# A graph-network kernel: what stands between encoder attention and the encoder MLP, rearranged

## The chip, the core and the metric

The kernel runs on one core of a Trainium2 chip. The metric is device time in microseconds (us) for one execution of the whole program. The core has five engines that run their own instruction streams and wait for each other through semaphores: TensorE (PE in the profile, with its weight loads as PEld), VectorE (DVE), ScalarE (ACT), GpSimd (POOL) and SyncE (SP). Here POOL and SP mostly issue DMA transfers. TensorE writes to PSUM, a small memory of eight banks, from which VectorE and ScalarE read.

## What is computed

Four graph layers run one after the other on 2708 nodes with 512 features each, with a dense 0/1 adjacency matrix; after each layer the input is added and a layer norm taken. The change lies in the first layer, and in a preparation for the fourth that is done in the middle of the first:

```
# layer 0 (cut)
Xw   = per head h (4 heads of 128): X_h @ W_h
att  = masked softmax of sigmoid(f1_i + f2_j), mask = adjacency
Xc   = att @ Xw                                  # encoder attention: "first pass"
Xn   = (Xc - mean) * rsqrt(var + 1e-6) * gamma + beta      # batch norm over the nodes
h    = elu(Xn @ Wm.T + bm) + Xn                  # encoder MLP
emb  = batch norm of h
Y    = att @ emb ...                             # decoder attention: "second pass"
# layer 3 (cut)
query, key = x @ Wq + bq, x @ Wk + bk
a    = query @ key.T / sqrt(512) + ...; softmax(a) @ value
```

Since a row of the softmax does not change when a constant is added to the row, layer 3 needs of its projections only the product M = Wq Wk^T / sqrt(512) and the vector u = Wk bq / sqrt(512).

## The kernel before, in words

All data is fp32. Features of layer 0 are held transposed, as `ft[128 features, 4 blocks, 2708 nodes]`. The two attention passes are written as `attention_pass`. Each has four parts (two halves of the nodes times two pairs of heads), and each part 22 steps, one for each block of 128 source nodes. A step forms a tile t of attention weights: two Tanh on ScalarE (L406, one for each head), a product with the mask on VectorE (L414), an Exp on ScalarE (L415). TensorE then multiplies: L438 in the first pass (22 small products for each step), L456 in the second. In the second pass some tiles are read back from DRAM instead of being formed, and VectorE counts zeros for some steps (L355). Two steps run ahead in the first pass; in the second, four tile buffers set how far the forming can run ahead.

At the end of each part of the first pass, `keep` (L636) divides the sums in PSUM by their row totals on VectorE (L656 to L658) into `rows`, and `turn` (L666) transposes the rows on TensorE (L675) into the banks of the second head of the pair. VectorE copies them into `ft` (L695), and later takes batch statistics of them (L697). The row totals are transposed as well (L683), copied (L685) and sent to DRAM as `rs_d` by POOL (L687, L691). SP reads them back as `rb` for the second pass (L333), after its `f1b` (L513). VectorE's first use of `rb` is `linked` (L884).

After the first pass the following is written down:

- `batch_scale` and `batch_shift` (L588, L602; the root is L111, on ScalarE) turn the statistics into `scale1` and `shift1`, so that Xn = scale1 * ft + shift1.
- Wq and Wk, loaded in two halves each by SP (L719), are transposed by TensorE in groups of four (L732) through two banks, psm0 and psm1, in turn. ScalarE copies each group into the end of `emb` (L737).
- `merged(c)` multiplies the transposed weights (L748); ScalarE scales and stores the result (L755). merged(0) comes first, 1 and 2 later. The fourth is made elsewhere.
- `small_product` (L608) multiplies a vector with a 512x512 matrix on TensorE as a row (L611), copies the row (L614), and turns it into a column (L616). It is called for `shift1` with the MLP weights (ps_shift), to give the MLP a bias that contains the shift, and for bq with Wk (ps_u), to give `uq`.
- The MLP weights `enc_w` are scaled in place by `scale1`, two blocks on VectorE (L777), two on ScalarE (L773). So the MLP reads the features before normalization.
- POOL writes the transposed weights and the merged product to DRAM (L781, L782, L786).

The MLP loop goes over six chunks of 452 or 450 nodes. For each chunk TensorE makes four output blocks of four products (L805) in pairs of banks, of which there are three. For each output block ScalarE takes an Exp (L575), VectorE makes the elu of it (L580, L582), adds `scale1 * ft` in place (L818; the rest of the shift is in the next batch norm, which removes any constant), and takes statistics (L821). Finished columns of `ft` are transposed by TensorE (L826) and copied to `emb` by ScalarE (L827).

The order on each engine is not the order of the text: a scheduler places the instructions by its own estimate of times, and each engine then works strictly in the order it was given. `tc.issue_after(x)` tells it to place an instruction after x. Waits on PSUM and SBUF are derived by tile. In the first pass a tile `both[q]` holds one bank of each of the two heads, so that the two banks are one tile to those waits; the fourth bank of each head is a tile by itself.

Of the kernel before, what the change touches and what calls it, by code (L numbers as in the profile page):

```python
# [8 lines left out]
F32 = mybir.dt.float32  # L9
# [3 lines left out]
AF = mybir.ActivationFunctionType  # L13
# [16 lines left out]
def gnn_stack_kernel(  # L30
# [149 lines left out]
    uq = const.tile([P, C], F32, name="uq")  # L180

    feats = ExitStack()
    pf = feats.enter_context(tc.tile_pool(name="feat", bufs=1, side="right"))
    with ExitStack() as l0:
# [36 lines left out]
        def project(att, psum):  # L221
# [90 lines left out]
            def rest(step):  # L312

                with tc.issue_after(step.ins):
# [8 lines left out]
                    copies(f2h[:, NT - 1, :])  # L323
                    nc.vector.tensor_scalar(bm1, prm_sb[:, MB_DEC, :], 1.0, None, ALU.subtract)

# [15 lines left out]
        def attention_pass(values, first, att, psum, finish, f1b=None, blocks=(), spread=None, rest=None):  # L341
# [23 lines left out]
            def form(hf, p, jt, att, prepare, f1b, tv):  # L365
# [49 lines left out]
                exp = nc.scalar.activation(tv, tv, AF.Exp, scale=0.5)  # L415
                if not opening:
                    opening[1] = tanh
# [182 lines left out]
        ready = [None]  # L600
# [7 lines left out]
        def small_product(ps, w, v, row):  # L608

            for c in range(C):  # L610
                nc.tensor.matmul(  # L611
                    ps[:1, :F], v[:, c : c + 1], w[:, c, :], start=(c == 0), stop=(c == C - 1)
                )
            nc.vector.tensor_copy(row, ps[:1, :F])  # L614
            for o in range(C):
                nc.tensor.matmul(  # L616
                    ps[:, o : o + 1],
                    row[:, o * P : (o + 1) * P],
                    ones[:1, 0:1],
                    start=True,  # L620
                    stop=True,
                )
            return ps[:, :C]


        stats = stats_tile("stats_a", 8)[:, :, : TURNS * NHALF]
        bias = p0.tile([P, 2, C], F32, name="enc_bias")
        with (
# [4 lines left out]
            mlp_w = []  # L633
            ft = feat_tile("ft")

            def keep(hf, p, po, later):  # L636
                h0, w = HSPAN[hf]
                if hf == 0 and p == 0:
                    mlp_w.append(load_mlp(enc_wT, "enc_w"))
                kept = []  # L640
# [25 lines left out]
                def turn(k):  # L666

                    h = HP * p + k
                    rows, rc = kept[k]
                    for b in range(TURNS):  # L670
                        slots = range(b * QUAD, min(NB, (b + 1) * QUAD))
                        bank = po[1][(TURNS * k + b) % (HB + 1)]
                        for r in slots:
                            i0, m = NODES[hf][r]
                            nc.tensor.transpose(  # L675
                                bank[:, r % QUAD * P : r % QUAD * P + m],
                                rows[:m, r, :],
                                ident[:m, :m],
                            )
                        c0 = b * BANK  # L680
                        cw = min(w, c0 + BANK) - c0
                        if b + 1 == TURNS:
                            nc.tensor.transpose(bank[:NB, BANK - P :], rc, ident)  # L683
                            sm = att.tile([NB, P], F32, tag="sm", name="sm")
                            nc.vector.tensor_copy(sm, bank[:NB, BANK - P :])  # L685
                            full = (NB - 1) * P
                            nc.gpsimd.dma_start(  # L687
                                rs_d[h, h0 : h0 + full].rearrange("(r i) -> r i", i=P),
                                sm[: NB - 1],
                            )  # L690
                            nc.gpsimd.dma_start(  # L691
                                rs_d[h : h + 1, h0 + full : h0 + w], sm[NB - 1 :, : w - full]
                            )
                        dst = ft[:, h, h0 + c0 : h0 + c0 + cw]
                        nc.vector.tensor_copy(dst, bank[:, :cw])  # L695
                        later.append(
                            lambda dst=dst, n=TURNS * hf + b: nc.vector.bn_stats(  # L697
                                stats[:, h, n, :], dst
                            )
                        )  # L700

                return [lambda k=k: turn(k) for k in range(HP)]

            attention_pass(xw, True, att, psum, keep, f1b, blocks, spread, rest)
            scale1, mean1 = batch_scale(stats, G_ENC, "bn1")
            shift1 = batch_shift(scale1, mean1, B_ENC, "bn1")


# [17 lines left out]
            for k, wt in enumerate((wqT, wkT)):  # L726
                for o in range(C):
                    slot = o % 2
                    tp = psum.tile([P, BANK], F32, tag=f"psm{slot}", name="tp_w", bufs=1)
                    tp = tp.rearrange("p (c d) -> p c d", c=C)  # L730
                    for c in range(C):
                        nc.tensor.transpose(  # L732
                            tp[:, c, :],
                            raws[2 * k + c // half][:, c % half, o * P : (o + 1) * P],
                            ident,
                        )
                    nc.scalar.copy(wt[:, o, :], tp.rearrange("p c d -> p (c d)"))  # L737
        with (
# [6 lines left out]
            def merged(c):  # L745
                ps = psum.tile([P, F], F32, tag="misc", name="ps_m", bufs=2)
                for o in range(C):
# [6 lines left out]
                    )  # L754
                nc.scalar.activation(mqk[:, c, :], ps, AF.Copy, scale=qscale)  # L755

            merged(0)


            (enc_w,) = mlp_w  # L760
# [22 lines left out]
            for c in range(1, C - 1):  # L783
                merged(c)
# [1335 lines left out]
```

## Time and profile before

| | us |
|---|---|
| median of 3 runs | 3179.41 (3178.1 to 3179.55) |
| profiled execution: device time | 3173.57 |
| profiled execution: span in the trace | 3171.7 |
| TensorE busy in the span | 3095.8 (98%) |
| VectorE busy | 2050.0 (65%) |
| ScalarE busy | 1347.0 (42%) |

The shares are means over stages that differ much. Layer 0 lies in the first 1090 us or so: the first attention pass ends at 522, the second begins at 644. What lies between is the subject here. A busy TensorE is not TensorE at its peak, since matmuls are pipelined; the granted clock (PEclk) and the weight loads tell more.

### The profile page before, as it was taken

Reading aid. Unit: us, or ns where it says so; the run is one execution under the profiler, and the core shown is the slowest. Engines: PE = TensorE matmul, PEld = TensorE weight load, DVE = VectorE, ACT = ScalarE, POOL = GpSimd, SP = SyncE. Lnnn points to the kernel's source line nnn. Section 1 sums busy time; section 2 is a strip of 40 time slices with the busy share of each in tenths; the row PEclk is TensorE's granted clock in tenths of the full one; section 3 lists DMA queues with packets and bytes.
Section 4 is the critical chain, followed back from the end, with each engine's and each line's share of the span. In section 5 each row is a group of like instructions: output and inputs, shape, how many; then the busy total and the mean of one; then the engine's idle time right before and its main releaser. Section 6 shows DMA issues by size and latency. Waiting matters only on the chain.

```text
span 3171.7 us, 39566 instructions
## 1 busy us (share of the span) xinstructions
PE 3095.8 (98%) x15176; PEld 2349.5 (74%) x15176; DVE 2050.0 (65%) x3819; ACT 1347.0 (42%) x1615; POOL 163.5 (5%) x282
## 2 busy tenths in 40 slices
PE   8899999999999999999999999999999999999999
PEld 7898897444444446885578888777768888888886
DVE  7968975776686684444167667767535555555565
ACT  7898896477867552001133333444301111111111
POOL 1101100000000000000011110000110000000000
PEclk9999999999999999999999999999999999999999
DMA  7866865156455413541154445566431111111111
GB/s 279 304 223 235 298 236 186 45 166 232 172 175 190 173 62 99 144 126 44 41 150 141 139 146 150 157 180 176 128 101 40 50 50 52 51 50 50 50 46 33
DMA packets 203635, 425.81 MB, mean 134 GB/s; under 512 B 20798, under 2 KB 134562, under 8 KB 197622
## 3 DMA queue, kind: packets, MB, share of 16 engines
q1 hardware_dynamic: 179454, 319.92, 33.0%
q0 software_dynamic: 23552, 101.26, 8.7%
q8 instruction: 119, 1.95, 0.2%
q10 hardware_dynamic: 440, 2.10, 0.2%
q14 instruction: 70, 0.57, 0.1%
HBM read 325.88 MB, written 95.87 MB: 133 GB/s over the span
## 4 chain that ended last, share of the span: by engine, by line
PE 77%; issue 11%; DVE 6%; ACT 3%; DMA 2%; POOL 1%; SPq 0%; POOLq 0%; DVEq 0%; ACTq 0%
PE po L1571 19%; PE ps_s L1366 18%; PE po L456 9%; PE ps_nb L1169 7%; PE po L438 7%; PE ps_wide L1219 4%; PE ps_sup L1777 2%; PE ps_mlp L805 2%; PE ps_hid L131 2%; DVE t L414 2%; PE ps_v L131 2%; PE ps_dec L936 2%; ACT t L406 1%; ACT t L415 1%; DMA kept<-t 1%
## 5 line engine op out<-in xcount | busy, mean ns | idle before, releaser
L414 DVE SCALAR_TENSOR_TENSOR t<-t,a 128x2708 f32<-128x2708 f32 (+1 forms) x152 | 450.4, 2975 | 175.3 <-ACT t L406 169.1
L438 PE MATMUL po<-xw,t 128*128 128x129 f32 (+2 forms) x3872 | 441.9, 280 | 36.3 <-ACT t L415 23.4
L438 PEld LDWEIGHTS po<-xw,t 128*128 128x128 f32 (+2 forms) x3872 | 434.1, 191 | 43.7 <-ACT t L415 35.2
L406 ACT ACTIVATE t<-f1b,f2h 128x1354 f32<-128x1354 f32 (+1 forms) x304 | 414.4, 1412 | 60.1 <-PE po L456 31.5
L1366 PE MATMUL ps_s<-q,hT 128*128 128x256 f32 (+1 forms) x1848 | 405.5, 372 | 0.0
L415 ACT ACTIVATE t<-t 128x2708 f32<-128x2708 f32 (+1 forms) x152 | 371.2, 2452 | 78.0 <-DVE t L414 75.4
L1571 PE MATMUL po<-sup,e 128*128 128x256 f32 (+1 forms) x1512 | 398.3, 384 | 5.6 <-DVE c L1652 2.8
L456 PE MATMUL po<-t,emb 128*128 128x452 f32 (+3 forms) x1056 | 396.2, 544 | 4.8 <-ACT t L415 4.7
L1366 PEld LDWEIGHTS ps_s<-q,hT 128*128 128x128 f32 x1848 | 339.2, 190 | 49.8 <-issue 5.1
L456 PEld LDWEIGHTS po<-t,emb 128*128 128x128 f32 (+1 forms) x1056 | 192.7, 189 | 201.5 <-issue 189.1
L1571 PEld LDWEIGHTS po<-sup,e 128*128 128x128 f32 (+1 forms) x1512 | 264.4, 185 | 59.9 <-issue 19.8
L1571 PE MATMUL po<-held,T 128*128 128x256 f32 x1200 | 293.7, 380 | 0.0
L1571 PEld LDWEIGHTS po<-held,T 128*128 128x128 f32 x1200 | 226.8, 190 | 31.4 <-issue 0.9
L1972 DVE SCALAR_TENSOR_TENSOR e<-a_cols,ps_s 128x512 f32<-128x512 f32 (+1 forms) x121 | 79.5, 657 | 233.5 <-PE ps_s L1366 229.8
L1366 PE MATMUL ps_s<-hT 128*128 128x256 f32 (+2 forms) x968 | 213.7, 372 | 0.7 <-ACT sup L1784 0.7
L1366 PEld LDWEIGHTS ps_s<-hT 128*128 128x128 f32 x968 | 174.9, 190 | 29.3 <-issue 4.4
L1169 PE MATMUL ps_nb<-hid_hi,at 128*128 128x512 f32 x484 | 185.5, 390 | 0.4 <-DVE at L1161 0.4
L1169 PE MATMUL ps_nb<-hid_lo,at 128*128 128x512 f32 x462 | 179.9, 389 | 0.0
L1874 ACT ACTIVATE a_score<-a_score,neg_big 128x512 f32<-128x512 f32 (+3 forms) x131 | 88.6, 683 | 194.5 <-DMA a_score<-in_adj_dram 94.2
L1476 ACT ACTIVATE e<-e 128x512 f32<-128x512 f32 (+1 forms) x187 | 113.8, 616 | 118.2 <-DVE e L1475 117.9
L1964 ACT ACTIVATE q<-ps_wide,uq 128x256 f32<-128x256 f32 (+1 forms) x44 | 20.5, 466 | 335.7 <-PE ps_wide L1219 335.7
L1571 PE MATMUL po<-sup,T 128*128 128x256 f32 x480 | 142.5, 380 | 0.0
(275 smaller groups left out, 3842.8 us busy)
## 6 DMA issues: line engine op xcount, KB each, us to landing
a<-adj_d SPq DMA_DIRECT2D x108, 677.0 KB
a_cols<-in_adjT_dram SPq DMA_DIRECT2D x200, 256.0 KB
a<-in_adjT_dram SPq DMA_DIRECT2D x42, 677.0 KB
adj_d<-a POOLq DMA_DIRECT2D x42, 677.0 KB, 5.9
kept<-t POOLq DMA_DIRECT2D x20, 1354.0 KB, 7.0
t<-kept SPq DMA_DIRECT2D x20, 1354.0 KB
raw<-in_adjT_dram SPq DMA_DIRECT2D x105, 256.0 KB
a_score<-in_adjT_dram SPq DMA_DIRECT2D x55, 256.0 KB
```

What stands on the lines that cost most here:

```text
L131: nc.tensor.matmul(ps[:n], xt[:, c, :n], w[:, c, :], start=(c == 0), stop=(c == C - 1))
L406: tanh = nc.scalar.activation(tv[:, k, :], f1b[k][:n, :w], AF.Tanh, bias=f2h[:n, jt, h : h + 1], scale=0.5,)
L414: step = nc.vector.scalar_tensor_tensor(tv, tv, GUARD, ab, ALU.add, ALU.mult)
L415: exp = nc.scalar.activation(tv, tv, AF.Exp, scale=0.5)
L438: nc.tensor.matmul(po[k][b][:m, s * DR : (s + 1) * DR], t[own : own + n, k, i0 : i0 + m], values[own : own + n, jt, HP * p + k, :], start= ...
L456: nc.tensor.matmul(po[HB * k + q][:, :qw], values[r : r + n, jt, h * P : (h + 1) * P], t[r : r + n, k, q0 : q0 + qw], start=(place == 0), ...
L1169: nc.tensor.matmul(pos[it][:n], at, half[:, jt, :], start=(jt == 0 and k == 0), stop=(jt == NT - 1),)
L1219: nc.tensor.matmul(ps[:, :width], w(c, o), xt(c), start=(c == 0), stop=(c == C - 1),)
L1366: nc.tensor.matmul(ps[:, jb, i:w], keys[:, c, j : j + P], st["q"][:, c, i:], start=(c == 0), stop=(c == C - 1),)
L1476: return nc.scalar.activation(e, e, AF.Exp)
L1571: nc.tensor.matmul(po[bank][rows, half, :], lhsT, rhs, start=(k == 0 and half == 0) if first is None else first, stop=last, skip_group_che ...
L1874: return nc.scalar.activation(a, a, AF.Identity, bias=neg_big[: a.shape[0]], scale=1.0e30)
```

## The change

It has five parts, all between the first attention pass and the MLP, with three small preparations earlier.

1. Features are normalized in place. ScalarE writes scale1 * ft + shift1 over `ft`, one chunk ahead of the MLP's matmuls (`normal`). The MLP's weights are no longer scaled, its bias is bm itself, `less` (bm - 1) is made at the start of the kernel, and the residual add becomes a plain add.
2. `small_product` is gone. VectorE computes `uq` by four products of Wk's rows with a broadcast bq, each with a sum over the row. bq is first written to DRAM by POOL, early in the first pass, and read back by SP with a broadcast, into a buffer of `f1b`.
3. The weight transposes use the four banks of the last part's first head, and stand in a fixed order with the last part's `turn`, which is cut into its three banks (`seam`). Three of the six feature copies of that part (those of the second head) go from VectorE to ScalarE.
4. `early_root` takes a root of a constant after the last Exp of the first pass.
5. The three merged products are made one after the other, before the MLP.

The same diff, cut to its core:

```diff
+    bq_d = dram.tile([C, P], F32, name="bq_d")
...
+                    nc.gpsimd.dma_start(bq_d.rearrange("c p -> p c"), prm_sb[:, Q_B, :])
                     nc.vector.tensor_scalar(bm1, prm_sb[:, MB_DEC, :], 1.0, None, ALU.subtract)
+                    nc.vector.tensor_scalar(less, prm_sb[:, MB_ENC, :], 1.0, None, ALU.subtract)
...
                 exp = nc.scalar.activation(tv, tv, AF.Exp, scale=0.5)
+                last_exp[:] = [exp]
...
-                def turn(k):
+                final = hf == NHALF - 1 and p + 1 == H // HP
+
+                def turn(k, b):
...
+                    copy = nc.scalar.copy if final and k + 1 == HP else nc.vector.tensor_copy
...
+                    copy(dst, bank[:, :cw])
...
+                if final:
+                    last_turn.append(turn)
+                    return []
...
-            scale1, mean1 = batch_scale(stats, G_ENC, "bn1")
-            shift1 = batch_shift(scale1, mean1, B_ENC, "bn1")
...
-            for k, wt in enumerate((wqT, wkT)):
-                for o in range(C):
-                    slot = o % 2
-                    tp = psum.tile([P, BANK], F32, tag=f"psm{slot}", name="tp_w", bufs=1)
...
+            bq = att.tile([P, HW], F32, tag="f1b", name="bq", bufs=HP + 1)
+            nc.sync.dma_start(
+                bq[:, :F], bq_d.rearrange("c p -> (c p)").partition_broadcast(P)
+            )
+            for c in range(C):
+                nc.vector.scalar_tensor_tensor(
+                    bq[:, F : 2 * F],
+                    raws[2 + c // half][:, c % half, :],
+                    qscale,
+                    bq[:, :F],
+                    ALU.mult,
+                    ALU.mult,
+                    accum_out=uq[:, c : c + 1],
+                )
+
+            def weights(k, o, b):
+                tp = last_po[0][b]
...
+                nc.scalar.copy((wqT, wkT)[k][:, o, :], tp)
+                return done
+
+            early_root = small.tile([P, 1], F32, tag="ready", name="early_root")
+            with tc.issue_after(last_exp[0].ins):
+                nc.scalar.activation(early_root, ones, AF.Sqrt)
+            banks4 = [HB] + list(range(HB))
+            turn = last_turn[0]
+            seam = [lambda o=o: weights(0, o, banks4[o]) for o in range(3)]
+            seam += [lambda: turn(0, 0), lambda: weights(0, 3, banks4[3])]
+            seam += [lambda: turn(0, 1), lambda: weights(1, 0, banks4[0])]
+            seam += [lambda: turn(0, 2), lambda: weights(1, 1, banks4[1])]
+            seam += [lambda: turn(1, 0), lambda: weights(1, 2, banks4[2])]
+            seam += [lambda: turn(1, 1), lambda: weights(1, 3, banks4[3])]
+            seam += [lambda: turn(1, 2)]
+            done = None
+            for work in seam:
+                with tc.issue_after(done.ins) if done else nullcontext():
+                    done = work()
+            for work in last_later[0]:
+                work()
+            scale1, mean1 = batch_scale(stats, G_ENC, "bn1")
+            shift1 = batch_shift(scale1, mean1, B_ENC, "bn1")
...
-            merged(0)
...
-            pm = small_product(
...
-            for c in range(1, C - 1):
+            for c in range(C - 1):
                 merged(c)
...
-            pu = small_product(
...
+            def normal(ci):
+                c0, w = CHUNKS[ci]
+                for c in range(C):
+                    cols = ft[:, c, c0 : c0 + w]
+                    nc.scalar.activation(
+                        cols,
+                        cols,
+                        AF.Identity,
+                        bias=shift1[:, c : c + 1],
+                        scale=scale1[:, c : c + 1],
+                    )
+
+            normal(0)
             turned = 0
             for ci, (c0, w) in enumerate(CHUNKS):
+                if ci + 1 < NCH:
+                    normal(ci + 1)
...
                     r = elu(
-                        att, pss[o][:, :w], w, bias[:, 0, o : o + 1], bias[:, 1, o : o + 1]
-                    )
-                    nc.vector.scalar_tensor_tensor(
-                        dst, dst, scale1[:, o : o + 1], r, ALU.mult, ALU.add
-                    )
+                        att, pss[o][:, :w], w, prm_sb[:, MB_ENC, o : o + 1], less[:, o : o + 1]
+                    )
+                    nc.vector.tensor_tensor(dst, dst, r, ALU.add)
                     nc.vector.bn_stats(stats[:, o, ci, :], dst)
```

## The prediction, made before the changed kernel was run

> **What bounds the kernel now.** I read the stage table first, then the order of time inside the stage that the change touches, then the waits. All times count from the start of the profiled execution. Busy time of each engine in four stretches (first attention pass, second half; the seam between it and the encoder MLP; the MLP; the start of the second pass):
>
> ```profile
> core 0: us, PE busy (x) PEld busy (x) DVE busy (x) ACT busy (x) POOL busy (x), PEclk, DMA share, GB/s
> 390.00:522.00 132.00, 126.71 (x1152) 125.55 (x1150) 86.46 (x89) 115.91 (x69) 6.83 (x13) 1.00 0.64 225
> 522.00:561.00 39.00, 33.04 (x110) 15.26 (x109) 23.94 (x53) 22.04 (x24) 5.79 (x10) 0.82 0.52 183
> 561.00:644.00 83.00, 82.82 (x272) 43.16 (x271) 63.50 (x97) 32.06 (x46) 0.57 (x1) 1.00 0.10 32
> 644.00:700.00 56.00, 55.63 (x165) 27.75 (x165) 41.63 (x41) 46.16 (x35) 1.05 (x2) 1.00 0.52 164
> ```
>
> TensorE is full before and after the seam. In the 39 us of the seam its clock averages 0.82, its weight loads fill only 15 us, and no engine is full: a chain of small steps. Because TensorE is full on both sides, every microsecond taken from the seam should end the kernel earlier. The seam in TensorE's own order:
>
> ```profile
> 522.22 0.60 PE L732 MATMUL tp_w<-ident,wq 128*128 128x128 f32 x4
> ...
> 530.73 1.11 PE L732 MATMUL tp_w<-ident,wq 128*128 128x128 f32 x4 [0.68 <-ACT emb L737]
> 532.52 1.12 PE L732 MATMUL tp_w<-ident,wk 128*128 128x128 f32 x4 [0.68 <-ACT emb L737]
> 534.31 1.11 PE L732 MATMUL tp_w<-ident,wk 128*128 128x128 f32 x4 [0.68 <-ACT emb L737]
> 536.30 5.90 PE L748 MATMUL ps_m<-emb 128*128 128x512 f32 x8 [0.88 <-ACT emb L737]
> 542.14 3.59 PE L611 MATMUL ps_shift<-enc_w,bn_shift 128*1 128x512 f32 x8
> 545.66 1.98 PE L748 MATMUL ps_m<-emb 128*128 128x512 f32 x4
> 548.68 1.05 PE L616 MATMUL ps_shift<-ones,emb 1*128 1x1 f32 x8 [1.04 <-DVE emb L614]
> 549.66 7.11 PE L748 MATMUL ps_m<-emb 128*128 128x512 f32 x12
> 556.71 3.59 PE L611 MATMUL ps_u<-emb,prm_sb 128*1 128x512 f32 x8
> 560.23 1.78 PE L805 MATMUL ps_mlp<-ft,enc_w 128*128 128x452 f32 x4
> 561.95 1.05 PE L616 MATMUL ps_u<-ones,emb 1*128 1x1 f32 x8
> 562.92 10.88 PE L805 MATMUL ps_mlp<-ft,enc_w 128*128 128x452 f32 x28
> ```
>
> Two small products stand on this path, with two records to each fp32 matmul. Transposes alternate with ScalarE copies in steps of 1.8 us. The first MLP matmul starts at 560.23, interrupted once for 0.97 (561.95 to 562.92), so the MLP starts in effect at 561.2. From there it runs without a gap to the first matmul of the second pass at 643.74: 82.5 us. ScalarE at the same place:
>
> ```profile
> 533.67 0.59 ACT L737 COPY emb<-tp_w 128x512 f32<-128x512 f32 x1 [1.21 <-PE tp_w L732]
> 534.28 1.28 ACT L111 ACT_TABLE_LOAD   x1
> 535.57 0.20 ACT L111 ACTIVATE bn_scale<-bn_scale 128x4 f32<-128x4 f32 x1
> ```
>
> VectorE had the variance ready at 533.1, and the root ended at 535.8, behind a copy and a table load; the shift was complete at 536.57.
>
> **What the Trainium skill says.** "TensorE: Matmul & The Clock Gate", Part 1, says an idle array drops to half clock and needs about 3.4 us of work to come back, and Part 4 says that transposes do not count as such work. The trace agrees: four transposes take 0.66 us at 529.40 but 1.11 at 530.73, and matmul records of L748 start 0.85 us apart until 540.7 and 0.43 after; between 551.1 and 554.5 they fall to 0.85 again, after the gap and the tiny matmuls at 547.6 to 549.7. "ScalarE: Activation LUTs", What ACT_TABLE_LOAD costs, gives 1283 ns for a load; its Table sets section says identity and copy are in every set. The trace shows 1.28 us and copies with no load around them. "PSUM — Partial Sum Buffer", PSUM bank collisions, says engines are kept apart on one bank even when both only read; the trace shows it as VectorE's L580 waiting 16.1 us in all for the Exp L575 on the same bank.
>
> **The change part by part.**
>
> Small products gone from TensorE. ps_shift: 3.59 + 1.05, with a wait of 1.04 before its second half; ps_u: 3.59 + 1.05. Together 10.3 us, all on the path. Their helpers on VectorE (L614 twice 0.67, the bias sums) and the enc_w scaling (0.49 twice on VectorE, 1.32 on ScalarE) go too.
>
> The query bias on VectorE: four products of 128x512 with an accumulator. The nearest row is L582 at 0.625 for 452, so I estimate 0.72 each, 2.9 in all. They stand after the memsets (512.02), before the normalization of the rows, and need the last wk load: issued at 509.14, and the DMA view in half-microsecond slices shows its 0.52 MB moving from 509.5 to 512.0. VectorE idles until 519.97, so 515 to 516 leaves 4 us spare: nothing. If the load came 4 us later it would cost one for one. The bq load on SP stands right behind a transfer issued at 385.61 and waits for the last Tanh on an old f1b buffer, which ended by 384.9; SP is idle afterwards until 400. Its 0.26 MB could hold the transfer that ScalarE waits for at 398.5 by 0 to 0.7; I take 0. The scattered write of bq_d (512 pieces of 4 bytes) falls in POOL's idle time before 37.63 (8.8 us); no row is like it; wqT_d, also 512 pieces, takes 0.75 to issue and 2.7 to land. Bounds 0 to 1.5; I take 0.
>
> Transposes over four banks. In the built program 11 ScalarE copies stand in a row (8 weights, 3 of features that VectorE loses). The waits are by tile, and a tile holds the banks of both heads, so the second weight group waits until VectorE has read the second head out of it (523.7 in the trace). Bounds: 522.9 plus 11 x 0.55 (start to start of L827's pairs) is 529.0; the old pace of 1.7 a copy would give 541. Walking the order with those waits, I get weights at 522.9, 524.3 and 524.95, then one copy every 0.55 to 0.6, the last at 530.8 because it waits for VectorE's small copy: it ends at 531.2. The first merged matmul then starts at 531.2 instead of 536.30.
>
> Scale and shift. VectorE loses three copies (1.6 start to start). Its unbroken chain ended at 532.97; I take 532.0, since it now waits for ScalarE's last copy. The early root has loaded the table in the idle time after the last Exp (514.5), so the rest is six small operations, 1.2 us: shift at 533.2 (before 536.57).
>
> Merged products back to back: 24 records, cold for 4.4 us (5 records at 0.85), 19 at 0.43: 12.5 us, so they end at 543.7. MLP matmuls start there instead of at 561.2: 17.5 us earlier. As a check: 10.3 removed, 5.1 earlier start, about 1.7 for the second cold stretch gone: 17.1.
>
> Normalization on ScalarE: 24 in-place Identity operations of 128x452. The nearest row is L1874, in place, biased, 0.72 for 512; I take 0.60 start to start (bounds 0.55 and 0.72). In the built order 21 of them and three 0.6 us copies of ps_m stand before the first Exp. Three normals end at 535.0; the first copy waits for the first merged product (537.2); then five, a copy, four, and the last copy when the merged products end (544.3); nine more to 549.7; the Exp table load 1.28; first Exp done 551.7. TensorE has the first chunk's features at 538.5, so it is not held there. VectorE waits: its first elu starts 8 us after TensorE's start, 7.3 before.
>
> VectorE in the MLP. Per output block 0.60 + 0.53 + 0.55 + 0.54 = 2.2 us (start to start; the add has no per-row scale now). Before, three second-pass products and two of their counts (2.9 and 1.56 us) were done ahead of the first elu, in the seam's gaps. Now all four products stand among the elus. TensorE's transposes of chunk 2 stand after the first half of chunk 3: 56 matmuls x 0.76 plus 7.75 blocks x 0.5 = 46.4, at 590.1. VectorE must by then have done 12 elus, three products and three counts: 26.4 + 8.7 + 4.7 = 39.8, so 591.5. That is 1.4 late, and about 1.5 more goes in small waits earlier (a chunk-1 add behind a count, a transpose buffer behind a Tanh). I take 3.0 us of TensorE stall; bounds 0 and 8.
>
> On POOL, wkT_d (1 MB) now goes ahead of the last row sums rs_d, and SP's f1b and rb wait for rs_d. Before, rb landed 10.9 us after its issue at 535.92. If rs_d lands by 536 to 541, rb lands at 545 to 552; the mask from it stands before the first elu: 0 to 2 us, inside the bound above.
>
> Sum: 17.5 - 3.0 = 14.5 us. The second pass starts with four tiles ready, as before, and is full on TensorE, so it keeps the gain. The profiled execution took 3173.57 (span 3171.7), so 3159.1; the median of the runs is 5.8 above it, so 3179.41 - 14.5 = 3164.9.
>
> **The rivals.**
> Little stall: the merged products stay at full clock (2.2 better) and VectorE keeps up. For it: the stages are balanced within 1.4 us. Against: clock falls at 530.7 in the trace. Gain 17 to 20, time 3161.
> VectorE as the bound of the MLP: normals at 0.72, a late rb, and Tanh pairs in front of Exps add up to 8 us of stall. For it: 76 us of VectorE work between first elu and end against 82.5 on TensorE, in an order fixed at build time. Against: the slack is regained in the last two chunks. Gain 9, time 3170.
> Slower: the first Exp behind the normals comes so late that TensorE stands still with its six banks full. It decides when the MLP loses more than 17.5 us; the first Exp would have to end at about 566, that is 0.68 us more for each of the 21 normals, 1.3 us each. Against: L1874 shows 0.72 for a longer row. Time then 3182.
> The gain is lost later: second-pass tiles late, TensorE waits at its start. The stretch 644 to 700 has ScalarE at 46 of 56 us, so it could take some, not all: time 3175.
>
> **How the numbers follow.** Forecast 0.52, little stall 0.17, VectorE bound 0.18, lost later 0.08, slower 0.05. A measurement of this kernel tells about 0.2%, 6.4 us, from no change; the first three cases lie beyond it: 0.87 less a little for tails, faster 0.86; lost later gives no change, 0.09; slower 0.05. The range takes in both ends of the unknown costs: 3159 to 3173.
>
> **What would show it.** L111 without a table load and the shift near 533; merged products in one run from about 531, once cold; the first MLP matmul near 544 and the first second-pass matmul near 629. The forecast is wrong if the MLP stretch is over 90 us, if TensorE waits for ScalarE before its first MLP matmul, or if the first attention pass ends later than 522.4.

## The result, and the profile after

The changed kernel takes 3167.33 us (median of 7 runs, 3162.98 to 3173.58), the kernel before 3178.10 (median of 7 in the same comparison, 3174.19 to 3179.72). The ratio of the means is 0.9969, with a 95% interval of 0.9959 to 0.9979: faster by 9.9 us, interval 6.7 to 13.0 (the medians lie 10.8 apart). The forecast was a gain of 14.5. The profiled execution took 3164.28 (span 3162.3), 9.3 less than the one before.

Both profiled executions have a clear mark: TensorE's first transpose of wq, when the first pass ends, at 522.22 before and 529.95 after. All intervals below are counted from it. First the stage table of the changed kernel (columns as in the forecast):

```profile
core 0: us, PE busy (x) PEld busy (x) DVE busy (x) ACT busy (x) POOL busy (x), PEclk, DMA share, GB/s
390.00:530.00 140.00, 133.61 (x1200) 132.41 (x1199) 96.53 (x102) 123.62 (x74) 8.44 (x16) 0.99 0.66 227
530.00:550.00 20.00, 17.63 (x83) 10.65 (x81) 10.31 (x35) 14.67 (x26) 3.32 (x6) 1.00 0.45 158
550.00:634.00 84.00, 82.36 (x263) 41.55 (x262) 69.13 (x102) 51.69 (x66) 3.32 (x4) 1.00 0.22 79
```

The seam took 39 us before; it takes 20 now, at a clock of 1.00 (0.82 before). The MLP has more ScalarE (51.7 us, before 32.1) and more VectorE in it, and TensorE is a little less full there. TensorE's own order in the timeline (start, duration, line, names, records; in brackets the idle time before it and what ended it):

```profile
529.95 0.60 PE L738 MATMUL po<-ident,wq 128*128 128x128 f32 x4
531.53 1.33 PE L738 MATMUL po<-ident,wq 128*128 128x128 f32 x8 [0.98 <-DVE rows L646]
...
537.69 0.27 PE L673 MATMUL po<-ident,rc 128*11 128x128 f32 x1
539.33 10.57 PE L776 MATMUL ps_m<-emb 128*128 128x512 f32 x24 [1.37 <-ACT ft L685]
549.73 12.30 PE L820 MATMUL ps_mlp<-ft,enc_w 128*128 128x452 f32 x32
...
563.25 0.44 PE L839 MATMUL tp_emb<-ident,ft 128*128 128x128 f32 x2 [0.24 <-DVE ft L833]
...
585.41 0.44 PE L839 MATMUL tp_emb<-ident,ft 128*128 128x128 f32 x2 [0.58 <-DVE ft L833]
...
594.18 0.44 PE L839 MATMUL tp_emb<-ident,ft 128*128 128x128 f32 x2 [0.35 <-DVE ft L833]
...
612.09 0.44 PE L839 MATMUL tp_emb<-ident,ft 128*128 128x128 f32 x2 [0.24 <-DVE ft L833]
...
634.22 3.27 PE L460 MATMUL po<-t,emb 128*128 128x452 f32 x8
```

Both small products are gone, the merged products are one run of 10.57 us, and the MLP starts at 549.73. Four short waits for VectorE's finished features (0.24, 0.58, 0.35, 0.24) and a few smaller ones stretch it to 84.5 us, where it had 82.5. From the mark to the first matmul of the second pass (643.74 before, 634.22 after): 121.52 us before, 104.27 after. So between these two profiles the place that was changed gave 17.25 us, while the whole gave 9.9.

The 17.25 rests on one profile of the kernel before. The run e4 below differs from that kernel only by one write in the first 40 us, so its profile shows the same seam a second time:

```profile
529.35 0.60 PE L734 MATMUL tp_w<-ident,wq 128*128 128x128 f32 x4
...
542.98 6.71 PE L750 MATMUL ps_m<-emb 128*128 128x512 f32 x8 [0.88 <-ACT emb L739]
...
648.44 3.27 PE L458 MATMUL po<-t,emb 128*128 128x452 f32 x8
```

From the mark to the second pass that is 119.09 us, 2.43 less. TensorE's clock fell once there; in the profile of the kernel before it fell a second time, from about 551 to 554.5. So the seam gave **14.8 to 17.25 us**, as much as forecast or more, and the whole gave less. In the first two profiles the rest is lost ahead of the mark, which comes 7.73 us later than before. Where, TensorE's and VectorE's timeline of the first 80 us show. The kernel before:

```profile
42.09 0.61 DVE L272 COPY f1c<-pf 128x450 f32<-128x450 f32 x1
45.17 2.98 DVE L414 SCALAR_TENSOR_TENSOR t<-t,a 128x2708 f32<-128x2708 f32 x1
...
73.42 15.36 PE L438 MATMUL po<-xw,t 128*128 128x129 f32 x132 [1.12 <-ACT t L415]
```

The changed kernel:

```profile
40.45 2.97 DVE L417 SCALAR_TENSOR_TENSOR t<-t,a 128x2708 f32<-128x2708 f32 x1
...
48.41 0.63 DVE L273 COPY f1c<-pf 128x450 f32<-128x450 f32 x1 [4.33 <-DMA f_d<-f1c]
...
49.09 5.62 PE L442 MATMUL po<-xw,t 128*128 128x129 f32 x48 [1.60 <-DVE f1c L273]
...
57.05 21.60 PE L442 MATMUL po<-xw,t 128*128 128x129 f32 x176 [2.34 <-ACT t L418]
...
79.77 10.57 PE L442 MATMUL po<-xw,t 128*128 128x129 f32 x89 [1.12 <-ACT t L418]
```

The third copy of f1c rows on VectorE now waits 4.33 us for a DMA, the write of the first f1c buffer to DRAM, because there are two such buffers, used in turn (a ring of two). Behind it on VectorE stands the next mask product, so ScalarE's Exp and then TensorE come late. The same resumption of TensorE, at 73.42 before, is at 79.77. About 1.4 of these 6.35 us are older than the wait: VectorE's first f1c copy already stands at 38.09 instead of 36.73. The DMA view from 24 to 60 us says what held that write (two rows of 40 slices: busy share of the DMA engines in tenths, and what they moved). The kernel before:

```profile
DMA  9878999999994986127999950692279993009489
GB/s 318 205 229 295 343 385 415 445 409 415 427 415 163 156 343 280 26 98 171 400 414 367 433 160 1 283 391 96 30 138 415 409 403 138 24 0 78 84 265 349
```

The changed kernel, and below it, from the same view of 20 to 60 us, its DMA issues on POOL's queue with their median time to landing:

```profile
DMA  9999999999999192179895357999995198006999
GB/s 376 205 234 229 283 367 403 427 409 433 415 415 410 50 72 6 12 60 48 42 48 30 24 78 274 396 378 392 401 380 148 47 417 355 12 0 108 379 433 403
```

```profile
f_d<-f1c POOLq DMA_DIRECT2D x2, 7.1 KB, 9.0
bq_d<-prm_sb POOLq DMA_DIRECT2D x1, 2.0 KB, 16.3
```

In the changed kernel eleven slices of 0.9 us, from 35.7 us on, move only 6 to 78 GB/s, at a share of up to 0.9. The suspect is the new write `bq_d`, 2 KB in 512 pieces of 4 bytes. It was issued at 29.40 and landed 16.3 us later, and the f1c writes issued behind it took 9.0 instead of 3.6. The trace's record of single DMA packets shows the order. The write's own data are 16 packets of 128 bytes, which run for 0.04 us each between 35.6 and 36.3 us. Right behind them packets of the adjacency loads, which SP issues on another queue, take up to 7.6 us (0.21 in the median, and at most 1.1 in the same stretch of the kernel before). The f1c packets run from 46.2 on. So loads of another queue are held as well as the f1c writes. "DMA: Bandwidth & Descriptors" of the Trainium skill fits in part: its Rules for kernel authors say that a strided last dimension becomes one descriptor for each element, and its section Two DMAs through the same engine are not ordered says that descriptors of one queue start in order on a DMA engine. The trace records packets, not descriptors; that the f1c packets come behind the write's agrees with the second, but the second does not explain why loads of another queue are held. That the write was the cause, and by which of several ways, was a matter for experiments.

### The profile page after: what moved, and what is told of

It is laid out like the page before. It is cut to its first block, busy times and chain, and to the rows that moved or that the text cites. A ratio compares the mean times of both kernels' runs of the same rounds, so it can differ in the third digit from the quotient of the medians.

```text
span 3162.3 us, 39537 instructions
## 1 busy us (share of the span) xinstructions
PE 3086.9 (98%) x15144; PEld 2348.9 (74%) x15144; DVE 2046.1 (65%) x3819; ACT 1361.8 (43%) x1640; POOL 163.2 (5%) x283
## 4 chain that ended last, share of the span: by engine, by line
PE 78%; DVE 7%; issue 7%; ACT 5%; DMA 3%; POOL 1%; SPq 0%; POOLq 0%; DVEq 0%; ACTq 0%
PE po L1584 21%; PE ps_s L1379 18%; PE po L460 9%; PE ps_nb L1182 7%; PE ps_wide L1232 5%; PE po L442 4%; PE ps_sup L1790 2%; PE ps_v L131 2%; ACT t L418 2%; PE ps_hid L131 2%; DVE t L417 2%; ACT t L409 2%; PE ps_dec L949 2%; PE ps_mlp L820 1%; PE ps_e L1512 1%
## 5 line engine op out<-in xcount | busy, mean ns | idle before, releaser
L442 PEld LDWEIGHTS po<-xw,t 128*128 128x128 f32 (+2 forms) x3872 | 436.5, 192 | 45.8 <-ACT t L418 35.6
```

The lines of the kernel that those rows point to most:

```text
L442: nc.tensor.matmul(po[k][b][:m, s * DR : (s + 1) * DR], t[own : own + n, k, i0 : i0 + m], values[own : own + n, jt, HP * p + k, :], start= ...
```

## Experiments

One profiled execution can't carry 7.7 us: runs of one kernel spread over up to 12.6 us (those of e2), and in the later profiles of kernels without the loss the mark lies anywhere from 523.5 to 530.8. Other transfers hold the first pass too: in e2 ScalarE waits 2.10 us for f1b before 32.15. So the early part is judged by times and by TensorE's resumption near 73 us. Counted from VectorE's first f1c copy, that resumption comes after 36.7 to 37.2 us in the ten profiles in which VectorE does not wait for f1c, and after 41.3 to 41.7 in the three in which it does. The seam is judged by its length from the mark, which for the changed seam repeats to 0.03 us (104.24 to 104.27 in six profiles).

**Is it the write?** Three kernels. e1 writes the query bias as four rows:

```diff
-nc.gpsimd.dma_start(bq_d.rearrange("c p -> p c"), prm_sb[:, Q_B, :])
+bank = psum.tile([P, BANK], F32, tag=f"psm{NCH % 2}", name="bq_t")
+nc.tensor.transpose(bank[:C, :P], prm_sb[:, Q_B, :], ident)
+bq_rows = p0.tile([C, P], F32, name="bq_rows")
+nc.vector.tensor_copy(bq_rows, bank[:C, :P])
+nc.gpsimd.dma_start(bq_d, bq_rows)
```

> The query bias reaches its row in memory as four rows of 512 bytes (one transpose of 128x4 on TensorE, one copy on VectorE, one write) instead of 512 pieces of 4 bytes; all else is the changed kernel. Theory A, the scattered write holds the DMA engines from about 36 to 45 us and so delays the first attention pass: no stretch of 9 us under 60 GB/s at high DMA share, VectorE's wait of 4.3 us at the third f1c copy gone, the first pass ends near 523 instead of 530.1, and the time is 6 to 7.5 us below the changed kernel's, a ratio to the kernel before near 0.9948. Theory B, the first 80 us vary from run to run or moved with the order of VectorE's small operations, and the write is harmless: the changed kernel's ratio again, 0.9969, and the first pass ends near 530.

Measured: 3161.25 us, ratio 0.9947 (0.9935 to 0.9959). VectorE doesn't wait, TensorE resumes at 74.00, and the write lands 2.2 us after its issue. The mark is at 527.56, later than theory A had it, within the spread named above. One thing more has changed, against the expectation: the write is issued at 46.29 instead of 29.40, behind the f1c writes. So e1 by itself does not tell whole rows from a later place.

e2 issues the scattered write 275 us later:

```diff
-nc.gpsimd.dma_start(bq_d.rearrange("c p -> p c"), prm_sb[:, Q_B, :])
...
+sums = nc.gpsimd.dma_start(
     rs_d[h : h + 1, h0 + full : h0 + w], sm[NB - 1 :, : w - full]
 )
+if (hf, p, k) == (0, 1, HP - 1):
+    with tc.issue_after(sums.ins):
+        nc.gpsimd.dma_start(bq_d.rearrange("c p -> p c"), prm_sb[:, Q_B, :])
```

> The same scattered write of 512 pieces of 4 bytes, issued about 275 us later, behind the softmax sums of the second part, at about 305 us. Theory A: the first 80 us run as in the kernel before (resumption near 73.4 instead of 79.8 us), and the stretch of low GB/s moves to 305 to 315 us; what it costs there is open, from 0 (TensorE has loads in hand) to the same 6 us; I take 1 to 2, a ratio near 0.9953. Theory B: the ratio 0.9969 and the late resumption at 79.8 stay.

Measured: 3161.50 us, ratio 0.9946 (0.9931 to 0.9961). No wait for f1c; TensorE resumes at 75.75, 37.2 us after VectorE's first f1c copy (which is late here, at 38.51, with no scattered write ahead of it). At 305.44 the write is issued, and a stretch of 0 to 22 GB/s shows from 309.8 to 315; TensorE's waits from 295 to 345 are 1.0 us in all, as in the changed kernel (3.8 in the kernel before). So the write in pieces slows the DMA engines at the later place too, but there it costs nothing that can be measured.

e4 is the kernel before with only this write added (unused):

```diff
+nc.gpsimd.dma_start(bq_d.rearrange("c p -> p c"), prm_sb[:, Q_B, :])
 nc.vector.tensor_scalar(bm1, prm_sb[:, MB_DEC, :], 1.0, None, ALU.subtract)
```

> The kernel before with nothing but the scattered write added, at the same place; nothing reads what it writes. Theory A: 6 to 7.7 us slower than the kernel before, ratio 1.0022, first pass ends near 529 to 530. Theory B: ratio 1.0000 within 0.0010, first pass ends near 522.

Measured: 3182.65 us (22 runs), before 3177.07 (29 runs), ratio 1.0016 (1.0010 to 1.0023): 5.1 us, interval 3.2 to 7.3. Its timeline:

```profile
46.64 0.63 DVE L273 COPY f1c<-pf 128x450 f32<-128x450 f32 x1 [4.47 <-DMA f_d<-f1c]
...
47.33 7.24 PE L440 MATMUL po<-xw,t 128*128 128x129 f32 x48 [3.21 <-DVE f1c L273]
...
78.00 12.23 PE L440 MATMUL po<-xw,t 128*128 128x129 f32 x104 [1.13 <-ACT t L417]
```

The wait of the changed kernel is there, and the resumption is 4.6 late, with the first f1c copy at 36.74, in place. Theory B is out.

**How does it cost time?** e3 doubles the write, to see whether its length is the price:

```diff
+nc.gpsimd.dma_start(bq_e.rearrange("c p -> p c"), prm_sb[:, Q_B, :])
 nc.gpsimd.dma_start(bq_d.rearrange("c p -> p c"), prm_sb[:, Q_B, :])
```

> The changed kernel with a second scattered write of the same 2 KB to another place, one behind the other at 29 us. Theory A: the DMA engines are held for about 18 us instead of 9, the first attention pass ends 6 to 9 us later again (536 to 539), ratio 0.9990. Theory B: the changed kernel's ratio, 0.9969, with the pass's end at 530.

A miss for theory A in its size: 3168.18 us, ratio 0.9972 (0.9961 to 0.9982), the changed kernel's. VectorE waits 4.8 us instead of 4.3, TensorE resumes at 78.44. What failed is the first step of the expectation: two writes did not hold the DMA engines for twice as long. Nine slices of 0.9 us, from 37.5 us on, move 6 to 128 GB/s, where one write had eleven. Packets of both writes had run by 36.3 us, as those of one. So this run does not tell what a longer hold would cost; why two hold no longer than one stays open. e5 leaves the write and gives the f1c rows a ring of their own with three buffers:

```diff
-f1c = att.tile([P, BW], F32, tag="rs", name="f1c")
+f1c = att.tile([P, BW], F32, tag="f1c", name="f1c", bufs=3)
```

> The changed kernel, scattered write left where it is, with three buffers instead of two for the f1c rows, so that VectorE's third copy needs no landed write. It tells apart two ways in which the scattered write can cost time. Theory A1, VectorE stands 4.3 us behind that one buffer and everything after it is late: the stretch of 9 us under 60 GB/s stays, but VectorE's wait is gone, TensorE resumes near 73.5 to 75 instead of 79.8, ratio near 0.9947. Theory A2, the held DMA engines delay the adjacency tiles and the rows that ScalarE needs, whatever VectorE does: resumption near 78 to 80 and the changed kernel's ratio, 0.9969.

Measured: 3159.75 us, ratio 0.9941 (0.9928 to 0.9953). DMA issues on POOL's queue, then VectorE and TensorE in the timeline of e5:

```profile
f_d<-f1c POOLq DMA_DIRECT2D x2, 7.1 KB, 10.6
bq_d<-prm_sb POOLq DMA_DIRECT2D x1, 2.0 KB, 14.6
```

```profile
42.10 0.61 DVE L273 COPY f1c<-pf 128x450 f32<-128x450 f32 x1
...
73.43 15.36 PE L442 MATMUL po<-xw,t 128*128 128x129 f32 x132 [1.12 <-ACT t L418]
```

The write is as slow as ever (14.6 us) and the f1c writes behind it too (10.6), but VectorE doesn't stop and TensorE is back at 73.43, the time of the kernel before. A1 holds, A2 falls: with the transfers delayed as much but VectorE not stopped, no loss shows; VectorE's stop at a ring of two buffers was the way in which the write cost time. e10 has both repairs:

> The changed kernel with both repairs: the query bias written as four rows of 512 bytes, and three f1c buffers. If one repair alone takes away all that the scattered write costs, the second adds nothing: 3160, ratio 0.9940 to 0.9947, TensorE's resumption at 73.4 to 74. If each took away a part, 3155 to 3158 and a ratio below 0.993.

It took 3163.92 us, ratio 0.9959 (0.9946 to 0.9971), with TensorE back at 74.17: no sign that the second repair adds anything. The ratio lies above the expected band. Its interval overlaps those of e1 and e5, and the changed kernel's as well, so by time alone e10 settles nothing. TensorE's resumption and the seam (104.25 us) are those of e1 and e5; I take the rest for spread of the first pass, which is not shown.

**What each part of the seam is worth.** Four kernels with the four-row write of e1, each with one part taken back. e6, two banks:

```diff
-banks4 = [HB] + list(range(HB))
+banks4 = [HB, 0, HB, 0]
```

> The query bias written as four rows of 512 bytes, as in e1, and the weight transposes over two banks instead of four, in the same order. Theory C, closely packed transposes keep TensorE's clock and gaps between them lose it: groups of four transposes wait for the copy before the last but one, gaps of 0.5 to 1.0 us come back, the clock falls before the merged products, which take 12.5 instead of 10.6 us, and first-pass end to first second-pass matmul grows from 104.1 to 109 to 112 us. Rival, ScalarE's copies set the pace of the seam in either case and the clock holds: 104 to 106 us. In time 3165 to 3169 against 3161 of e1, or the same.

Measured: 3163.61 us, ratio 0.9948 (0.9933 to 0.9963), mark to second pass 107.10 us, 2.8 more. In length between the two expectations; the clock falls, as theory C has it. TensorE in the timeline, then a stage table of 4 us around the start of the merged products:

```profile
532.89 0.66 PE L742 MATMUL po<-ident,wq 128*128 128x128 f32 x4 [0.85 <-DVE rc L649]
...
537.40 0.66 PE L742 MATMUL po<-ident,wk 128*128 128x128 f32 x4 [0.81 <-ACT ft L689]
...
539.29 12.26 PE L780 MATMUL ps_m<-emb 128*128 128x512 f32 x24 [0.84 <-ACT ft L689]
```

```profile
536.00:540.00 4.00, 2.35 (x16) 1.64 (x15) 3.01 (x8) 2.37 (x5) 1.96 (x4) 0.98 0.17 49
540.00:544.00 4.00, 4.00 (x7) 1.55 (x6) 0.96 (x6) 2.28 (x4) 0.53 (x2) 0.59 0.67 264
```

Gaps of 0.85 and 0.81 are back, and the clock, 1.00 until about 540, averages 0.59 in the next 4 us: 12.26 us for the merged products instead of 10.57, so 1.7 us; they also start 1.4 later after the mark, and the MLP is 0.3 shorter. In all ten profiles with four banks the clock stays 1.00 from the mark to the second pass; in all three with two banks (the kernel before, e4, e6) it falls, 8 to 11.5 us after the mark. The later start is a rival to the gaps. Against it stands e9 below: its first product after the transposes starts 11.7 us after the mark, later than here, and the clock stays 1.00. That is one profile; the gaps were not varied alone.

e7, no early root:

```diff
-with tc.issue_after(last_exp[0].ins):
-    nc.scalar.activation(early_root, ones, AF.Sqrt)
```

> As e1, without the early root on ScalarE, so that the root of the scale loads its table itself. As forecast: 1.3 us of table load move behind the last feature copy, the shift comes 1.3 us later, and the first MLP matmul 0 to 1.3 us later, since the merged products cover the shift: shift complete near 12.6 after the pass's end instead of 11.3, first normal and first elu 1.3 later, 104.1 becomes 104.1 to 105.4. Rival: no difference at all, since the merged products end 8 us after the shift.

Measured: 3162.19 us, ratio 0.9948 (0.9935 to 0.9962), mark to second pass 104.02 us. The rival is right, and more: even the root is only 0.2 later after the mark (10.63 instead of 10.45), since the table load runs in the 1.12 us that ScalarE otherwise waits for VectorE's variance. The early root is worth nothing here.

e8, the query bias on TensorE (small_product of the kernel before, called after the merged products). Against what its expectation says, the four rows of e1 are still written to memory, but nothing reads them:

```diff
-bq = att.tile([P, HW], F32, tag="f1b", name="bq", bufs=HP + 1)
...
-    nc.vector.scalar_tensor_tensor(
...
+pu = small_product(psum.tile([P, F], F32, tag="misc", name="ps_u", bufs=2), wkT,
+                   prm_sb[:, Q_B, :], emb[:1, NT - 3 * C - 2, :])
+nc.scalar.activation(uq, pu, AF.Copy, scale=qscale)
```

> The changed kernel with the query bias taken back to TensorE, as the small product of the kernel before, behind the merged products; no bias row in memory, no scattered write, no products on VectorE. As forecast the small product costs TensorE 3.6 + 1.05 us on the path: 104.1 becomes 108.5 to 109, the first pass ends as in e1 (523 to 528), time 4.6 above e1: 3165 to 3166, ratio near 0.9962. Rival: TensorE waits in the MLP for VectorE anyway (2.0 us of stall), so that part of the 4.6 is hidden: 106.5 to 107, ratio near 0.9955.

Measured: 3168.45 us, ratio 0.9965 (0.9953 to 0.9977), mark (530.78) to second pass 108.55 us: 4.3 more. TensorE:

```profile
540.15 10.57 PE L782 MATMUL ps_m<-emb 128*128 128x512 f32 x24 [1.37 <-ACT ft L706]
550.65 3.59 PE L619 MATMUL ps_u<-emb,prm_sb 128*1 128x512 f32 x8
554.17 1.78 PE L834 MATMUL ps_mlp<-ft,enc_w 128*128 128x452 f32 x4
555.89 1.05 PE L624 MATMUL ps_u<-ones,emb 1*128 1x1 f32 x8
...
639.33 1.00 PE L464 MATMUL po<-t,emb 128*128 128x452 f32 x2
```

The 3.59 and 1.05 stand on the path as forecast; little of them is hidden.

e9, weights scaled instead of features normalized (the block of the kernel before from `row` to the scaling of `enc_w`, the old elu bias and the old last product; `normal` removed):

```diff
+pm = small_product(
+    psum.tile([P, F], F32, tag="misc", name="ps_shift", bufs=2),
+    enc_w, shift1, row[:, 1, :],
+)
...
-if ci + 1 < NCH:
-    normal(ci + 1)
...
-nc.vector.tensor_tensor(dst, dst, r, ALU.add)
+nc.vector.scalar_tensor_tensor(dst, dst, scale1[:, o : o + 1], r, ALU.mult, ALU.add)
```

> As e1, with the normalization taken back to the way of the kernel before: the encoder weights scaled by VectorE and ScalarE, the shift through the weights as a small product on TensorE, the scale in the last product of each elu block; no feature is normalized on ScalarE. As forecast: the small product (3.6 + 1.05 us) returns and stands ahead of the merged products, which then wait for the shift (about 2 us later than their start in e1), but VectorE's first elu starts about 7 us earlier and the MLP's 2.0 us of stall go. First transpose to first second-pass matmul: 104.3 + 4.65 + 1 to 2 - 2 = 108 to 109, time 3165 to 3166 where e1 has 3161, ratio near 0.996. Rival, the normals on ScalarE cost as much as they save: 104 to 105.5, ratio 0.9947.

Measured: 3167.05 us, ratio 0.9968 (0.9956 to 0.9980), mark (526.91) to second pass 108.71 us, 4.4 more, as forecast. TensorE:

```profile
538.62 3.59 PE L619 MATMUL ps_shift<-enc_w,bn_shift 128*1 128x512 f32 x8 [3.70 <-DVE bn_shift L613]
...
553.72 14.57 PE L845 MATMUL ps_mlp<-ft,enc_w 128*128 128x452 f32 x38
...
635.62 3.27 PE L464 MATMUL po<-t,emb 128*128 128x452 f32 x8
```

The small product waits 3.70 us for the shift, and the merged products wait behind it. The MLP itself, 81.9 us, has no stall. So the normals cost 2.6 in the MLP and save 7 in front of it.

The four parts taken back one at a time make 2.8 - 0.2 + 4.3 + 4.4 = 11.3 us. The seam gave 14.8 to 17.25; what is left belongs to what no run took back alone, such as the three merged products in one run and the feature copies on ScalarE, and to what the parts do together.

e11 is e10 with ScalarE's normals held back:

```diff
 if ci + 1 < NCH:
-    normal(ci + 1)
+    with tc.issue_after(first_exp.ins) if ci else nullcontext():
+        normal(ci + 1)
```

Here `first_exp` is the first Exp of the chunk before ci. 

> As e10, and ScalarE's normalizations of chunk 2 and later are held behind the first Exp two chunks earlier, so that 8 of them stand ahead of the first Exp instead of 21. Theory D, the 2.0 us of TensorE stall in the MLP come from VectorE's late start behind those 21: first Exp about 6 us earlier, the stall falls to 0 to 0.5, first transpose to first second-pass matmul 102.3 to 102.8 instead of 104.3, time 1.5 to 2 below e10. Rival, VectorE's order in the MLP is what is late: 104 again; or the held normals come late and TensorE waits for features of chunk 2 or 3: above 104.3.

Measured: 3160.09 us, ratio 0.9944 (0.9932 to 0.9957), mark (523.54) to second pass 102.97 us, 1.3 less than e10. The order of ScalarE, then TensorE, in the timeline:

```profile
550.70 0.61 ACT L585 ACTIVATE elu_m<-ps_mlp,prm_sb 128x452 f32<-128x452 f32 x1
...
543.32 13.05 PE L827 MATMUL ps_mlp<-ft,enc_w 128*128 128x452 f32 x34
...
569.36 0.41 PE L848 MATMUL tp_emb<-ident,ft 128*128 128x128 f32 x2 [0.19 <-DVE ft L842]
...
580.34 0.44 PE L848 MATMUL tp_emb<-ident,ft 128*128 128x128 f32 x2 [0.54 <-DVE ft L842]
...
626.51 3.27 PE L464 MATMUL po<-t,emb 128*128 128x452 f32 x8
```

The first Exp starts 7.4 us after the first MLP matmul instead of 8.3, so hardly earlier: four Tanh of the second pass (5.37 us) took the place of the normals. The waits are fewer and later (0.19, 0.54), and the MLP takes 83.2 us. Theory D holds in direction, by the length of the seam (the times of e10 and e11 have overlapping intervals); its "6 us earlier" was a miss. e5 and e11 are faster than both kernels: their intervals end at 0.9953 and 0.9957, the changed kernel's begins at 0.9959.

## Why the prediction was right, and where it was wrong

In words of the forecast, with all its times counted from its mark 522.2:

| step | forecast | measured |
|---|---|---|
| merged products start after the mark | 9.0 | 9.4 |
| shift complete | 11.0 | 11.5 |
| merged products, until the MLP starts | 12.5 | 10.4 |
| first MLP matmul | 21.5 | 19.8 |
| first Exp done | 29.5 | 28.7 |
| stall in the MLP | 3.0 | 2.0 |
| mark to second pass, gain | 14.5 | 14.8 to 17.25 |
| scattered write of bq_d | 0 (0 to 1.5) | 5.1 (3.2 to 7.3) |

**The failed step: "Bounds 0 to 1.5; I take 0"** for the write of bq_d. The forecast saw that POOL is idle when the write is issued, and took wqT_d (also 512 pieces, 2.7 us to land) as a bound. POOL was idle indeed: the instruction took 0.79 us and delayed nothing on POOL. But the count of pieces was the wrong likeness (those of wqT_d have 512 bytes each), and the idle time of the issuing engine the wrong question. While the write was under way the f1c writes did not land, and VectorE needs one of them landed to reuse its buffer. In the kernel before, they landed 3.6 us after issue and VectorE never waited there, so no wait in the trace pointed to the place. A gain of 14.8 to 17.25 in the seam less 5.1 makes 9.7 to 12.2; 9.9 was measured, with an interval of 6.7 to 13.0. The 7.7 us by which the mark moved in the two profiles is more than the write explains: the profiled execution before lies 3.5 below the median of 29 later runs of that kernel (3177.07).

**Luck.** The time was forecast as 3164.9 and measured as 3167.33. In gain that is 9.9 instead of 14.5. The time came nearer than the gain because the kernel before was itself 1.3 faster in this comparison (3178.10 against 3179.41), and the gain came as near as it did because the errors have opposite signs: the write cost 5.1 more than the forecast, and the seam gave 0.3 to 2.75 more.

**Right.** The order of the seam's chain, and most of its steps: the copies over four banks and the shift to 0.5 us, the first Exp to 0.8. The query bias on VectorE was hidden: four products of 0.69 and a read of the accumulator of 0.08 each, where I had 0.72, and VectorE was idle afterwards:

```profile
520.58 0.69 DVE L725 SCALAR_TENSOR_TENSOR bq<-wk,bq 128x512 f32<-128x512 f32 x1 [0.82 <-DMA wk<-in_wk_dram]
...
523.40 0.08 DVE L725 DVE_READ_ACCUMULATOR bq<-wk,bq 128x1 f32 x1
527.70 0.16 DVE L644 TENSOR_SCALAR rc<-po 128x1 f32<-128x1 f32 x1 [4.22 <-PE po L442]
```

It waited 0.82 for the last wk load, and 4.22 were left over; the forecast had 4 us spare. The rb transfer and VectorE's `linked` were no hindrance: the first elu came later than both.

**Mis-sized.** The merged products: the forecast let the clock fall as in the kernel before, 8 us after the last matmul of the first pass. After the change they started 9.4 us after the mark at full clock; 2.1 us better. That was the first rival ("merged products stay at full clock"), in half: the other half, that VectorE keeps up, did not come true. Part 4 of "TensorE: Matmul & The Clock Gate" of the Trainium skill says that transposes do not count as work for the clock. The changed kernel does not show this: 6.4 us of unbroken transposes (531.5 to 538.0, between gaps of 0.98 and 1.37) left it at 1.00 for the merged products. The stall: 2.0 for 3.0, and e9 and e11 show that it hangs on ScalarE's normals. The early root was costed as a help to the shift only, and rightly added nothing to the sum.

**The signs.** "The first attention pass ends later than 522.4" came true, but it could not tell: the mark comes later than that, at 523.5 to 530.8, in every profile without the loss too, except that of the kernel before itself, which has the earliest mark of all (522.22). It led to the right place by luck.

## What to carry to other kernels

Price a DMA by the size of its pieces and by what has to land while it is under way, not by its bytes or by the idle time of the engine that issues it; then ask which buffer ring waits for those transfers. Three ways took the cost away here: the write in pieces at a later time (e2), whole rows by way of one transpose, issued behind the f1c writes (e1), and a third buffer (e5). Whether another queue would have done it was not tried; SP's loads were held as well. When a local gain is confirmed and the total falls short, compare the two traces from the start of the program. Judge by marks that repeat between executions, and take a second profile of the kernel before too: its seam was 2.4 us shorter the second time.

## What the runs showed of the hardware

- A write of 2 KB in 512 pieces of 4 bytes took 16.3 us to land (14.6 in e5). Its own packets ran in 0.7 us; behind them the DMA engines moved 6 to 78 GB/s for 9.9 us, and packets of loads on another queue took up to 7.6 us instead of 0.21. As four rows of 512 bytes, issued 17 us later, it landed in 2.2.
- Two such writes, one behind the other, held the next write no longer than one did (VectorE's wait 4.8 us against 4.3 and 4.5). Why they do not add up stays open.
- After 6.4 us of transposes without a gap TensorE's clock was still 1.00, in e9 even after 3.70 us of idle time behind them. With gaps of 0.8 among them it averaged 0.59 in the 4 us after 540.
- One program's seam can differ by 2.4 us between two executions (121.52 and 119.09) by where the clock falls and how often.
- A table load of 1.28 us on ScalarE cost 0.2 where the engine had 1.12 us to wait anyway.
